# A graph network on one core: queries, edge weights and running sums in SBUF, and a table built in pairs of PSUM banks

## The chip, the core and the metric

One of the eight cores of a Trainium2 chip runs the whole program. Its engines each work through a queue of their own in order: PE (matrix products), DVE (vector work), ACT (copies and functions of single elements), POOL (here it issues the DMAs whose addresses come from a list of rows, and nothing else of weight) and SP (plain DMAs). Products land in PSUM, 8 banks of 512 float32 for each of 128 partitions; the rest of the working data lies in SBUF. The metric is the device time of one execution in microseconds. Three runs of the kernel before took 4051.14, 4055.07 and 4069.09 us; the median is 4055.07.

## What is computed

Two layers of a heterogeneous graph transformer over 6250 nodes of 16 types and 100000 edges of 32 types, with 8 heads of 16, and then a residual layer norm:

```python
def gt_layer(x, ntype, etype, src, dst, Wk, Wq, Wv, Wa, Watt, Wmsg, pri, skip, g, b):
    k, q, v = (typed_linear(x, ntype, W).reshape(n, H, HS) for W in (Wk, Wq, Wv))
    kT = jnp.einsum('nhd,htdo->nhto', k, Watt)
    vT = jnp.einsum('nhd,htdo->nhto', v, Wmsg)
    a = jnp.einsum('ehd,ehd->eh', kT[src, :, etype], q[dst]) * pri[:, etype].T / SQRT_D
    att = edge_softmax(a, dst, n)
    hag = segment_sum((vT[src, :, etype] * att[:, :, None]).reshape(-1, H * HS), dst, n)
    h = silu(typed_linear(hag, ntype, Wa))
    alpha = sigmoid(skip[ntype])[:, None]
    return layernorm(h * alpha + x * (1 - alpha)) * g + b
out = layernorm(x + (gt_layer(gt_layer(x)) @ ff_w + ff_b))
```

## The kernel before

**The table.** For each layer a table in device memory holds, for every node and each of the 32 edge types, a row of 256 numbers: the node's key and value turned by that type's matrices. An edge then needs one row, (source node, edge type), of 1 KB.

**The stages.** First the nodes are ranked by type and number of incoming edges, in 50 blocks of 128 nodes, while PE builds the first layer's table. Then `edges(0)` runs over superblocks of 3 or 4 blocks: for every block it gathers the rows of its edges, does the attention and sums up, and `nodes` turns the sums into the layer's output. From this output `nodes` makes keys, values and queries of layer 2, and `pieces_of` with `table_block` builds the second layer's table block by block, beside the gathers of later superblocks. Last, `edges(1)` does the same over the second table, with the final layer norm in `nodes` and no table beside it. The other branch, `arm(False)`, handles graphs that don't fit the blocks; it doesn't run here.

**One block of edges.** Rows come in chunks of four edges for each of 128 nodes. POOL issues four gathers for a chunk (L970) into one of twelve `kv` buffers. DVE multiplies the key half by the query (L982), sums it by heads into `a` (L986), and, once all chunks are in, `finished` subtracts the maximum, ACT takes the exponential (L894), and DVE sums the weights (L897), multiplies the value halves by them (L905) and adds the products up in `acc` (L912), which L915 sums over its four slots. `finished` of one block is interleaved with the chunks of the next.

**What lies in PSUM.** For these steps three operands are kept in PSUM: a `qw` tile in one bank (two buffers) holds a block's query, which ACT copies there (`query`, L876), and behind it the weights that ACT writes; `acc` has a bank of its own. Two banks (`nps`) serve the node work and three (`tps`) the tiles `tb` of the table. That is all eight.

**One block of the table.** `table_block` makes, for 16 edge types at a time, a staging tile `st` out of two halves, keys and values. A half is four products, one for each pair of heads, with 32 rows of PE each and 512 columns, each into a bank `tb` of its own; PE does each product in two instructions (L261). ACT copies each bank to `st` (L268); in the last superblock DVE does copies 1 and 3 (L266). When both halves are there, POOL scatters `st` to the table (L1188), three steps later in the program. Each half ends in a `yield`, at which other work is interleaved.

**What sets the order.** The program is written by generators: after each chunk, `tick` advances the node work (`work`) and the table (`pieces`) by as many steps as `spread` planned for the chunk. POOL's queue is kept in the order in which this is written, gathers and scatters mixed. The other engines' queues are put in order by a scheduler, which goes by when it expects operands to be ready. A gather waits for its `kv` buffer to be free, a scatter for ACT's (or DVE's) copies, and layer 2's first gather for all scatters.

Of the kernel before, what the change touches and what calls it, by code (L numbers as in the profile page):

```python
# [18 lines left out]
P = 128  # L19
# [77 lines left out]
def kernel(  # L97
# [54 lines left out]
    typed = dram.tile([NB, P], I32, name="typed")  # L152
# [97 lines left out]
    def table_block(pool, ps_pool, kT, vT, i, share, bufs, store):  # L250


        for tg in range(TG):
            tt = slice(tg * 16, (tg + 1) * 16)
            st = pool.tile([P, 16, 2 * D], F32, name="st", bufs=bufs)
            for half, (yT, bd) in enumerate(((kT, bdk), (vT, bdv))):
                for hp in range(HP):
                    s = slice(hp * 2 * HS, (hp + 1) * 2 * HS)
                    pt = ps_pool.tile([P, SB * P], F32, name="tb").rearrange(
                        "p (t c) -> p t c", t=16)  # L260
                    nc.tensor.matmul(pt, yT[s, i * P:(i + 1) * P], bd[s, tt, :],  # L261
                                     start=True, stop=True)
                    c0 = half * D + hp * 2 * HS
                    to = st[:, :, c0:c0 + 2 * HS]
                    if hp in share:
                        nc.vector.tensor_copy(to, pt)  # L266
                    else:
                        nc.scalar.copy(to, pt)  # L268
                yield
            store(tg, st)  # L270
# [168 lines left out]
    with tc.tile_pool(name="tp", bufs=2) as tp, \  # L439
# [4 lines left out]
        def rank_order():  # L444
# [204 lines left out]
            tyr = pp.tile([NB, P], I32, name="tyr")  # L649
# [119 lines left out]
    def arm(fast):  # L769
# [65 lines left out]
        def edges(l):  # L835
# [38 lines left out]
            def query(s, i):  # L874
                qw = qwp.tile([P, 512], F32, name="qw")
                nc.scalar.copy(qw[:, :D], got[s][0][:, i, :])  # L876
                return qw

            def finished(s, i, chunks, kvt, a, w, sums, den):
# [14 lines left out]
                nc.scalar.activation(w, av, AF.Exp)  # L894
                yield
                yield
                nc.vector.tensor_reduce(den[:, i, :], w.rearrange("p k h -> p h k"),  # L897
                                        axis=AX.X, op=ALU.add)

                acc = accp.tile([P, CH, D], F32, name="acc")  # L900
                for j in range(len(chunks) + 1):
                    if j < len(chunks):
# [5 lines left out]
                            w[:, j0:j1, :].unsqueeze(3).to_broadcast([P, j1 - j0, H, HS]),  # L908
# [29 lines left out]
            qw = query(0, 0)  # L938
            for s, (i0, k, types) in enumerate(sbs):
# [6 lines left out]
                for i in range(k):  # L946
# [17 lines left out]
                    for j0, j1 in chunks:  # L964
# [3 lines left out]
                        for j in range(j0, j1):  # L968
# [14 lines left out]
                            kk, kk, qw[:, :D].unsqueeze(1).to_broadcast([P, c, D]), op=ALU.mult)  # L983
# [14 lines left out]
                    w = qw[:, D:D + K * H].rearrange("p (k h) -> p k h", h=H)  # L998
                    before = finished(s, i, chunks, kvt, a, w, sums, den)
                    qw = then[0] if then else None  # L1000
# [60 lines left out]
        def nodes(l, i0, k, types, sums, den, ntb, table):  # L1061
# [46 lines left out]
            if not last:  # L1108
# [49 lines left out]
                table(pieces_of(i0, k, outs[0], outs[1], (1, 3) if final else ()))  # L1158
# [23 lines left out]
        def pieces_of(i0, k, kT, vT, share):  # L1182
# [182 lines left out]
```

## Time and profile before

| what | value |
|---|---|
| median of 3 runs | 4055.07 us |
| the profiled execution's own time | 4025.79 us |
| its span | 4024.0 us |
| mean granted PE clock | 0.67 |
| busy: PE, DVE, ACT, POOL | 2266.9, 2184.1, 910.9, 1947.0 us |
| gathers (L970) | 1734 |
| scatters of the second table (L1188) | 100 |

Times are microseconds from the span's start. A row of the timeline has start, duration, engine, line, operation, output and inputs, the number of like instructions in a row, and in brackets the engine's idle time before it with what ended that. A row of waits has who waited for whom, then the total, the number of waits and the longest. A row of stretches has, for each engine, its busy time and (x) its instructions, then the granted PE clock, the DMA engines' busy share and what they moved. A row of a group has its number, its busy time, the mean ns of one, and the idle time of the engine just before them.

### The profile page before, as it was taken

How to read it: one execution, taken by the hardware profiler on the slowest of the kernel's cores; microseconds unless marked ns; L12 is line 12 of the kernel's file. 1: busy time of each engine (PE TensorE's matmuls, PEld its weight loads, DVE VectorE, ACT ScalarE, POOL GpSimd, SP SyncE). 2: the span in 40 equal slices, each digit the busy share in tenths (PEclk: the TensorE clock that was granted, in tenths of full speed). 3: DMA queues.
4: the chain of work that ended last, by engine and by line, in shares of the span. 5: the costliest groups of instructions: out<-in, count | busy, mean ns of one | idle time of the engine just before them, and what ended most of it. 6: DMA issues, size and time to landing. Idle time of an engine off the chain costs nothing. (4 is left out here: it accounts for less than half of the span.)

```text
span 4024.0 us, 26100 instructions
## 1 busy us (share of the span) xinstructions
PE 2266.9 (56%) x7142; PEld 1031.4 (26%) x7142; DVE 2184.1 (54%) x4912; ACT 910.9 (23%) x1854; POOL 1947.0 (48%) x2032
## 2 busy tenths in 40 slices
PE   4999998930675578877878889701112112012312
PEld 2444553310232223323333334301111011001111
DVE  4787783335545456545635744244654565555645
ACT  1443434520242123422333245300000000000000
POOL 0000015446465545565455654175666665765663
PEclk9999999955665667666766765555555555555555
DMA  5676647983374435764566567533333332332321
GB/s 137 278 308 273 256 203 307 359 253 93 127 251 163 153 117 206 275 204 147 191 240 213 181 230 273 230 107 90 90 100 92 89 103 86 103 96 86 95 86 44
DMA packets 201152, 697.87 MB, mean 173 GB/s; under 512 B 61332, under 2 KB 110616, under 8 KB 175946
## 3 DMA queue, kind: packets, MB, share of 16 engines
q0 software_dynamic: 105424, 448.83, 33.6%
q1 hardware_dynamic: 72924, 237.40, 15.1%
q10 hardware_dynamic: 22642, 9.82, 1.0%
q8 instruction: 60, 0.98, 0.1%
q14 instruction: 102, 0.84, 0.1%
HBM read 271.40 MB, written 429.49 MB: 174 GB/s over the span
## 5 line engine op out<-in xcount | busy, mean ns | idle before, releaser
L970 POOL DMA_INDIRECT kv<-tab,ell x1734 | 1659.3, 957 | 820.2 <-issue 502.7
L268 ACT COPY st<-tb 128x512 f32<-128x512 f32 x1364 | 740.8, 591 | 978.0 <-PE tb L261 695.8
L261 PE MATMUL tb<-bdv,kvT 32*128 32x512 f32 x800 | 450.3, 988 | 105.8 <-issue 74.2
L261 PE MATMUL tb<-bdk,kvT 32*128 32x512 f32 x800 | 428.1, 960 | 64.9 <-ACT st L268 34.6
L982 DVE TENSOR_TENSOR kv<-kv,qw 128x512 f32<-128x512 f32 (+3 forms) x468 | 297.6, 640 | 306.9 <-DMA kv<-tab,ell 255.1
L731 PE MATMUL l<-xm,wkqv 128*128 128x512 f32 (+1 forms) x832 | 388.0, 601 | 55.9 <-DVE xm L232 54.4
L247 PE MATMUL nb<-ident,hag 128*128 128x128 f32 x100 | 27.6, 418 | 670.2 <-DVE hag L1019 267.6
L1188 POOL DMA_INDIRECT tab<-st,row x100 | 101.3, 1013 | 479.9 <-ACT st L268 413.1
L986 DVE TENSOR_REDUCE a<-kv 128x32 f32<-128x512 f32 (+3 forms) x468 | 296.3, 638 | 64.8 <-remote 35.0
L232 DVE SCALAR_TENSOR_TENSOR xm<-ntb,nb 128x384 f32<-128x384 int32 (+1 forms) x336 | 186.2, 593 | 255.1 <-PE nb L247 163.4
L247 PE MATMUL nb<-ident,hs 128*128 128x128 f32 x100 | 35.4, 458 | 426.0 <-DVE hs L1099 156.1
L912 DVE TENSOR_TENSOR acc<-kv,acc 128x512 f32<-128x512 f32 (+3 forms) x368 | 234.3, 637 | 65.0 <-remote 46.6
L241 PE MATMUL nb<-xm,wa 128*128 128x384 f32 (+1 forms) x384 | 218.3, 729 | 71.6 <-DVE xm L232 27.4
L905 DVE TENSOR_TENSOR kv<-kv,qw 128x512 f32<-128x512 f32 (+3 forms) x368 | 228.1, 627 | 0.0
L266 DVE COPY st<-tb 128x512 f32<-128x512 f32 x220 | 151.1, 687 | 135.5 <-PE tb L261 100.0
L731 PEld LDWEIGHTS l<-xm,wkqv 128*128 128x128 f32 x832 | 149.5, 194 | 288.9 <-issue 201.3
L261 PEld LDWEIGHTS tb<-bdv,kvT 32*128 32x128 f32 x800 | 147.7, 268 | 292.7 <-issue 153.2
L232 DVE SCALAR_TENSOR_TENSOR xm<-ntb,hT 128x512 f32<-128x512 int32 (+1 forms) x208 | 133.9, 658 | 137.8 <-PE l L731 105.9
L261 PEld LDWEIGHTS tb<-bdk,kvT 32*128 32x128 f32 x800 | 146.0, 261 | 235.6 <-ACT st L268 138.4
L247 PEld LDWEIGHTS nb<-ident,hag 128*128 128x128 f32 x100 | 16.5, 207 | 694.2 <-issue 515.1
L719 POOL DMA_DIRECT2D ntb<-in_node_type_dram x13 | 7.3, 560 | 342.5 <-DVE xm L232 342.5
L261 PE MATMUL tb<-bdv,yT 32*128 32x512 f32 x784 | 169.8, 662 | 3.3 <-ACT st L268 2.3
(235 smaller groups left out, 2633.0 us busy)
## 6 DMA issues: line engine op xcount, KB each, us to landing
tab<-st SPq DMA_DIRECT2D x98, 2048.0 KB
kv<-tab,ell POOLq DMA_INDIRECT x1734
ntb<-typed SPq DMA_DIRECT2D x20, 192.0 KB
hr<-xrd SPq DMA_DIRECT2D x20, 192.0 KB
xrd<-xr POOLq DMA_DIRECT2D x11, 256.0 KB
hr<-in_x_dram POOLq DMA_DIRECT2D x10, 256.0 KB
ntb<-in_node_type_dram POOLq DMA_DIRECT2D x10, 256.0 KB
ntb<-typed SPq DMA_DIRECT2D x10, 256.0 KB
```

Of the source, the lines that this page charges most:

```text
L232: nc.vector.scalar_tensor_tensor(xm[:, :n], ntb[:, :n], float(t), hT[:, :n], op0=ALU.is_equal, op1=ALU.mult)
L241: nc.tensor.matmul(ps[:, :n], w[:, t, :], xm[:, :n], start=(t == types[0]), stop=(t == types[-1]))
L261: nc.tensor.matmul(pt, yT[s, i * P:(i + 1) * P], bd[s, tt, :], start=True, stop=True)
L266: nc.vector.tensor_copy(to, pt)
L268: nc.scalar.copy(to, pt)
L731: nc.tensor.matmul(ps[i][:, :n], wkqv[:, i, t, :], xm[:, :n], start=(t == 0), stop=(t == TY - 1))
L905: nc.vector.tensor_tensor((v if j else acc).rearrange("p k (h d) -> p k h d", h=H), v.rearrange("p k (h d) -> p k h d", h=H), w[:, j0:j1, ...
L912: nc.vector.tensor_tensor(acc[:, :j1 - j0], kvt[j - 1][:, :j1 - j0, D:], acc[:, :j1 - j0], op=ALU.add)
L970: get = nc.gpsimd.indirect_dma_start(out=kv[:, j - j0, :], out_offset=None, in_=tabs[l][:], in_offset=bass.IndirectOffsetOnAxis(ap=ell[:, ...
L982: nc.vector.tensor_tensor(kk, kk, qw[:, :D].unsqueeze(1).to_broadcast([P, c, D]), op=ALU.mult)
L986: nc.vector.tensor_reduce(a[:, j0:j1, :], kk.rearrange("p k (h d) -> p k h d", h=H), axis=AX.X, op=ALU.add)
L1188: put = nc.gpsimd.indirect_dma_start(out=tabs[1].rearrange("(n t) c -> n (t c)", t=16), out_offset=bass.IndirectOffsetOnAxis(ap=row2[:, tg ...
```

## The change

The query is read where it lies in SBUF, and `query` no longer copies it; the weights are written over the logits in `a`, in SBUF; `acc` is an SBUF tile. Three banks of PSUM come free. `tps` stays at three buffers, but in the second layer's table (`w=2`) each is now a pair of banks: two products fill it, and one copy of 128x1024 empties it. In the last superblock DVE takes the second pair of each half in place of copies 1 and 3. The node types `typed`, `tyr` and `ntb` (used in the masks of the typed linear layers) become bf16 in place of int32, half the bytes. The first layer's table (`w=1`, pool `tnb` of five banks) and the branch for other graphs keep single banks.

```diff
-    typed = dram.tile([NB, P], I32, name="typed")
+    typed = dram.tile([NB, P], BF16, name="typed")
...
-    def table_block(pool, ps_pool, kT, vT, i, share, bufs, store):
+    def table_block(pool, ps_pool, kT, vT, i, share, bufs, store, w=1):
...
-                for hp in range(HP):
-                    s = slice(hp * 2 * HS, (hp + 1) * 2 * HS)
-                    pt = ps_pool.tile([P, SB * P], F32, name="tb").rearrange(
-                        "p (t c) -> p t c", t=16)
-                    nc.tensor.matmul(pt, yT[s, i * P:(i + 1) * P], bd[s, tt, :],
-                                     start=True, stop=True)
+                for hp in range(0, HP, w):
+                    pt = ps_pool.tile([P, w, SB * P], F32, name="tb").rearrange(
+                        "p b (t c) -> p b t c", t=16)
+                    for b in range(w):
+                        s = slice((hp + b) * 2 * HS, (hp + b + 1) * 2 * HS)
+                        nc.tensor.matmul(pt[:, b], yT[s, i * P:(i + 1) * P], bd[s, tt, :],
+                                         start=True, stop=True)
                     c0 = half * D + hp * 2 * HS
-                    to = st[:, :, c0:c0 + 2 * HS]
+                    to = st[:, :, c0:c0 + w * 2 * HS].rearrange("p t (b c) -> p b t c", b=w)
...
-        if fast:
-            qwp = ctx2.enter_context(tc.tile_pool(name="qwp", bufs=2, space=PSUM))
-            accp = ctx2.enter_context(tc.tile_pool(name="accp", bufs=1, space=PSUM))
...
-            ntb = npl.tile([P, SB * P], I32, name="ntb", bufs=3)
+            ntb = npl.tile([P, SB * P], BF16, name="ntb", bufs=3)
...
             def query(s, i):
-                qw = qwp.tile([P, 512], F32, name="qw")
-                nc.scalar.copy(qw[:, :D], got[s][0][:, i, :])
-                return qw
+                return got[s][0][:, i, :]
...
-                nc.scalar.activation(w, av, AF.Exp)
+                nc.scalar.activation(av, av, AF.Exp)
...
-                nc.vector.tensor_reduce(den[:, i, :], w.rearrange("p k h -> p h k"),
+                nc.vector.tensor_reduce(den[:, i, :], av.rearrange("p k h -> p h k"),
...
-                acc = accp.tile([P, CH, D], F32, name="acc")
+                acc = ep.tile([P, CH, D], F32, name="acc", bufs=1)
...
-                            w[:, j0:j1, :].unsqueeze(3).to_broadcast([P, j1 - j0, H, HS]),
+                            av[:, j0:j1, :].unsqueeze(3).to_broadcast([P, j1 - j0, H, HS]),
...
-                            kk, kk, qw[:, :D].unsqueeze(1).to_broadcast([P, c, D]), op=ALU.mult)
+                            kk, kk, q.unsqueeze(1).to_broadcast([P, c, D]), op=ALU.mult)
...
-                table(pieces_of(i0, k, outs[0], outs[1], (1, 3) if final else ()))
+                table(pieces_of(i0, k, outs[0], outs[1], (2,) if final else ()))
...
-                yield from steps(table_block(ep, tps, kT, vT, i, share, STB, store))
+                yield from steps(table_block(ep, tps, kT, vT, i, share, STB, store,
+                                             2 if fast else 1))
```

POOL's queue holds the same instructions in the same order as before. On the other engines the rows below show what stands there now; the changed kernel's lines are a few off those of before (its L269 is the copy L268, its L262 the product L261, its L890 the exponential L894, its L978, L982, L901 and L908 are L982, L986, L905 and L912).

ACT's queue in layer 1, from one exponential to the next, before (`st<-tb` are the copies of the table, the rest is node work):

```order
L894 ACTIVATE qw<-a 128x120
L268 COPY st<-tb 128x16x32 x6
L876 COPY qw<-q 128x128
L1146 COPY kvT_7794<-nb 128x384
L1146 COPY kvT_7804<-nb 128x384
L812 COPY qT<-nb 128x384
L268 COPY st<-tb 128x16x32
L816 COPY q<-nb 128x384
L268 COPY st<-tb 128x16x32 x5
L812 COPY qT<-nb 128x512
L268 COPY st<-tb 128x16x32 x4
L894 ACTIVATE qw<-a 128x112
```

And the same place now:

```order
L890 ACTIVATE a<-a 128x120
L269 COPY st<-tb 128x2x16x32 x3
L1141 COPY kvT_7704<-nb 128x384
L1141 COPY kvT_7714<-nb 128x384
L810 COPY qT<-nb 128x384
L814 COPY q<-nb 128x384
L269 COPY st<-tb 128x2x16x32 x3
L810 COPY qT<-nb 128x512
L269 COPY st<-tb 128x2x16x32 x2
L890 ACTIVATE a<-a 128x112
```

Sixteen copies became eight of twice the size, the copy of a query is gone, and a copy of the table that stood between two copies of node work has moved behind them.

PE's queue in layer 1, a little later, before (`tb` are the table's products, `hs` the transposes of a superblock's output, `wkqv` the products of keys, values and queries from it):

```order
L261 MATMUL tb<-bdv,kvT_7804 128x512 x4
L261 MATMUL tb<-bdk,kvT_7794 128x512 x3
L247 MATMUL nb<-ident,hs 128x128 x2
L261 MATMUL tb<-bdk,kvT_7794 128x512
L261 MATMUL tb<-bdv,kvT_7804 128x512 x4
L247 MATMUL nb<-ident,hs 128x128
L261 MATMUL tb<-bdk,kvT_7794 128x512
L1141 MATMUL nb<-xm,wkqv 128x384 x8
L261 MATMUL tb<-bdk,kvT_7794 128x512 x3
L1141 MATMUL nb<-xm,wkqv 128x384 x4
```

And now:

```order
L262 MATMUL tb<-bdv,kvT_7714 128x512 x4
L262 MATMUL tb<-bdk,kvT_7704 128x512 x4
L262 MATMUL tb<-bdv,kvT_7714 128x512 x4
L247 MATMUL nb<-ident,hs 128x128 x3
L262 MATMUL tb<-bdk,kvT_7704 128x512 x2
L1136 MATMUL nb<-xm,wkqv 128x384 x8
L262 MATMUL tb<-bdk,kvT_7704 128x512 x2
L1136 MATMUL nb<-xm,wkqv 128x384 x4
```

Halves that were cut into three products and one, or one and three, with other work between them, now stand whole or as two and two; nothing else moved far.

DVE's queue in layer 2, at the end of a superblock, where the next superblock's first query is needed (the multiplication by it stands first), before:

```order
L982 TENSOR_TENSOR kv<-kv,qw 128x4x128 [waits DMASW6_49,DMASW5_49,DMASW7_49,DMASW4_49,Activation_49]
L912 TENSOR_TENSOR acc<-kv,acc 128x128 [waits DVE_49]
L885 TENSOR_TENSOR a<-a,neg 128x96
L915 TENSOR_REDUCE sums<-acc 128x128 [waits DVE_49]
L986 TENSOR_REDUCE a<-kv 128x32
L890 TENSOR_REDUCE m<-a 128x8 [waits DVE_49]
```

And now:

```order
L978 TENSOR_TENSOR kv<-kv,q 128x4x128 [waits DMASW7_49,DMASW6_49,DMAHW5_49,DMASW5_49,DMASW4_49]
L908 TENSOR_TENSOR acc<-kv,acc 128x128 [waits DVE_49]
L881 TENSOR_TENSOR a<-a,neg 128x96
L911 TENSOR_REDUCE sums<-acc 128x128 [waits DVE_49]
L982 TENSOR_REDUCE a<-kv 128x32
L886 TENSOR_REDUCE m<-a 128x8 [waits DVE_49]
```

The order is the same; the multiplication no longer waits for ACT's copy of the query but for the query's own load (DMAHW5), beside the four gathers.

More of the change, by code (lines that the diff above doesn't have):

```diff
@@ L648, in rank_order @@
             yield
-            tyr = pp.tile([NB, P], I32, name="tyr")
+            tyr = pp.tile([NB, P], BF16, name="tyr")
             nc.vector.tensor_copy(tyr, ty_ps)
@@ L874, in query, with finished @@
             def query(s, i):
-                qw = qwp.tile([P, 512], F32, name="qw")
-                nc.scalar.copy(qw[:, :D], got[s][0][:, i, :])
-                return qw
-            def finished(s, i, chunks, kvt, a, w, sums, den):
+                return got[s][0][:, i, :]
+            def finished(s, i, chunks, kvt, a, sums, den):
                 i0, k, _ = sbs[s]
@@ L937, in edges @@
             before = iter(())
-            qw = query(0, 0)
+            q = query(0, 0)
             for s, (i0, k, types) in enumerate(sbs):
@@ L997, in edges @@
                         step(end=True)
-                    w = qw[:, D:D + K * H].rearrange("p (k h) -> p k h", h=H)
-                    before = finished(s, i, chunks, kvt, a, w, sums, den)
-                    qw = then[0] if then else None
+                    before = finished(s, i, chunks, kvt, a, sums, den)
+                    q = then[0] if then else None
             for _ in before:
```

## The prediction

> **What bounds the kernel now.** I read the table of stretches first, then POOL's waits, then the timeline of one half of a table.
>
> ```profile
> core 0: us, PE busy (x) PEld busy (x) DVE busy (x) ACT busy (x) POOL busy (x), PEclk, DMA share, GB/s
> 1040.00:2500.00 1460.00, 1152.00 (x2595) 494.13 (x2596) 764.07 (x1744) 474.48 (x945) 785.64 (x811) 0.66 0.57 200
> 2500.00:2604.00 104.00, 90.57 (x207) 39.56 (x204) 31.36 (x73) 37.49 (x71) 11.79 (x12) 0.58 0.61 246
> 2604.00:4024.00 1420.00, 256.81 (x642) 146.81 (x642) 779.87 (x2082) 57.42 (x174) 876.71 (x916) 0.53 0.31 91
> ```
>
> The three stretches are the steady part of layer 1's edges (with the second layer's table built beside them), its tail, and layer 2's edges. The change leaves the first 1040 us nearly alone. POOL issues every gather, and its cadence is this:
>
> ```profile
> 1637.54 0.94 POOL L970 DMA_INDIRECT kv<-tab,ell  x1 [0.30 <-issue]
> 1649.43 1.01 POOL L1188 DMA_INDIRECT tab<-st,row  x1 [10.94 <-ACT st L268]
> ...
> L970 POOL DMA_INDIRECT kv<-tab,ell x1734 | 1659.3, 957 | 820.2 <-issue 502.7 <-DVE acc L905 121.2 <-DMA tab<-st 52.6
> ```
>
> A gather takes 0.95 us and 0.30 us pass before the next: 1.25 us. In the steady part 811 instructions need 785.64 + 811 x 0.30 = 1029 us of 1460, so 431 us are waits. In layer 2, 916 need 1152 of 1420.
>
> ```profile
> POOL tab L1188 <- ACT st L268: 362.2, 51, 42.5
> POOL kv L970 <- DVE gi L1032: 31.9, 1, 31.9
> POOL kv L970 <- DVE acc L905: 27.4, 4, 21.7
> POOL tab L1188 <- ACT qw L876: 14.2, 4, 7.0
> ```
>
> So in the steady part the waits are nearly all one thing: POOL stands at a scatter of the table (L1188), with all later gathers behind it in its queue, until ACT has emptied the banks. (The second column is the total, then the number, then the longest.) In layer 2 the row of another kind stands:
>
> ```profile
> POOL out_dram L1220 <- DVE o L1174: 97.7, 11, 26.9
> POOL kv L970 <- DVE acc L905: 93.8, 11, 18.2
> ```
>
> There POOL waits for DVE some 190 us, no table is built, and POOL's own cadence sets the rest. Why is ACT late in layer 1? One half (four products of 32 rows, eight PE instructions, two for a product):
>
> ```profile
> 1649.51 2.08 PE L261 MATMUL tb<-bdk,kvT 32*128 32x512 f32 x6
> 1651.61 1.56 ACT L268 COPY st<-tb 128x512 f32<-128x512 f32 x3 [2.46 <-PE tb L261]
> 1652.25 2.07 PE L261 MATMUL tb<-bdk,kvT 32*128 32x512 f32 x2 [0.66 <-ACT st L268]
> 1654.36 0.59 ACT L268 COPY st<-tb 128x512 f32<-128x512 f32 x1 [1.18 <-PE tb L261]
> ```
>
> Three banks take three products side by side in 2.08 us; the fourth has no bank until ACT has emptied one, and then takes as long alone as the three did. PE is held from 1649.51 to 1654.32, ACT done at 1654.95. The mean over the steady part, for this line alone:
>
> ```profile
> 1040.00:2500.00 1460.00, 681.19 (x1439) 258.90 (x1440) 0.66 0.57 200
> 2500.00:2604.00 104.00, 72.32 (x163) 29.70 (x160) 0.58 0.61 246
> ```
>
> 1439 instructions are 180 halves, 3.79 us each; 20 halves in the tail, 3.55 each. PE, 79% busy in its own order, is what ACT and then POOL wait for.
>
> **The change, part by part.** *Pairs of banks.* Now three tiles of two banks: six products fit, so the four of a half run side by side, and the next half's first pair has a place as well. ACT empties a pair at once; no copy of 1024 is in the trace, but these two are:
>
> ```profile
> L1146 ACT COPY kvT<-nb 128x384 f32<-128x384 f32 x16 | 7.7, 479 | 52.7 <-PE nb L1141 41.1 <-issue 8.6 <-remote 3.1
> L1146 ACT COPY kvT<-nb 128x512 f32<-128x512 f32 x8 | 4.7, 586 | 45.7 <-PE nb L1141 25.5 <-remote 20.2
> ```
>
> 128 more elements cost 107 ns, so 1024 cost 586 + 428 = 1014 ns, against two copies of 0.59. A half then holds PE no less than the 2.08 us that six instructions take and ACT 2.03 us; no more than the 3.79 of now. Both ends of the pipe stand near 2.1, so I take 2.3: 180 x 1.49 = 268 us less of PE's queue in the steady part. What this is worth is read at POOL: a scatter needs two halves. If only its own halves count, 51 waits get 2 x 1.49 = 3.0 us shorter, 153 us; if the backlog ahead of them goes as well, all 362.2 + 14.2 = 376 us go. I take **-250 us**, a little under the middle. In the tail, 20 halves by 3.55 - 2.3 = **-25 us**, since PE is busy there for 90.57 of 104. What comes next as a bound in layer 1 is POOL's 1029 us.
>
> *Query copies go, exp stays in SBUF.* A hundred ACT copies (L876) and their waits go.
>
> ```profile
> DVE den L897 <- ACT qw L894: 146.6, 25, 31.8
> DVE kv L982 <- DMA kv<-tab,ell: 128.4, 34, 13.4
> DVE kv L982 <- ACT qw L876: 37.2, 3, 18.0
> ```
>
> These DVE waits shrink (ACT stood behind PE, as above), but DVE is then early for gathers that POOL has not issued: POOL waited for DVE's buffers only 27.4 us (L905) here. Priced 0; between -59 (these 27.4 and the one wait of 31.9) and 0. The query's buffer is now held until DVE's last multiplication, not until ACT's copy: behind its load stand SP's loads of types and old rows. It has two buffers and is asked for a superblock ahead, so 0; without that lead DVE would wait as for L876, 37.2. *Types as bf16* halves loads that are also issued a superblock ahead, hidden behind its gathers: 0, and no wait shown here is for them. The last superblock's copies on DVE (one pair of two instead of copies 1 and 3) carry the same data: 0.
>
> *Operands from PSUM to SBUF.* Four groups change their source or target:
>
> ```profile
> L982 DVE TENSOR_TENSOR kv<-kv,qw 128x512 f32<-128x512 f32 (+3 forms) x468 | 297.6, 640 | 306.9 <-DMA kv<-tab,ell 255.1 <-ACT qw L876 37.2 <-issue 13.9
> L912 DVE TENSOR_TENSOR acc<-kv,acc 128x512 f32<-128x512 f32 (+3 forms) x368 | 234.3, 637 | 65.0 <-remote 46.6 <-issue 11.7 <-DVE kv L905 4.0
> L905 DVE TENSOR_TENSOR kv<-kv,qw 128x512 f32<-128x512 f32 (+3 forms) x368 | 228.1, 627 | 0.0
> L905 DVE TENSOR_TENSOR acc<-kv,qw 128x512 f32<-128x512 f32 x100 | 68.4, 684 | 0.0
> L580 DVE TENSOR_TENSOR rl<-oc,shifts 128x512 f32<-128x512 f32 x10 | 6.8, 682 | 0.0
> L583 DVE TENSOR_TENSOR oc<-oc,ps 128x512 f32<-128x512 f32 x10 | 6.8, 680 | 2.5 <-PE ps L576 2.5
> ```
>
> Their own duration stays: with both inputs in SBUF (L580) 682 ns, with one in PSUM (L583) 680. [...]
>
> What the move does cost stands in POOL's rows. All 1304 now read two operands from SBUF, and where an instruction of that kind runs today, a gather that starts beside it is longer:
>
> ```profile
> 1655.51 0.56 DVE L1019 TENSOR_TENSOR hag<-sums,rd 128x384 f32<-128x384 f32 x1
> 1655.78 1.10 POOL L970 DMA_INDIRECT kv<-tab,ell  x1 [0.30 <-DVE sums L915]
> 2282.05 2.10 DVE L232 SCALAR_TENSOR_TENSOR xm<-ntb,h 128x512 f32<-128x512 int32 x3
> 2282.05 2.10 POOL L970 DMA_INDIRECT kv<-tab,ell  x1 [0.30 <-issue]
> 3062.94 0.86 DVE L1095 SCALAR_TENSOR_TENSOR hs<-hs,mv,gt 128x128 f32<-128x128 f32 x3
> 3063.29 1.07 POOL L970 DMA_INDIRECT kv<-tab,ell  x1 [0.30 <-issue]
> ```
>
> The first gather met L1019 with 0.29 us of it left and lost 0.15 (1.10 against 0.95): the rest of the DVE instruction less 0.14. The second lost 1.15 behind two that followed each other; the third slipped in behind one of three short ones and lost 0.12. [...]
>
> The four groups hold 297.6 + 234.3 + 228.1 + 68.4 = 828.4 us, 414 for each layer, 29% of layer 2's 1420 us. If starts fall at random and a gather gets in behind the first instruction of 0.68 us, a hit loses 0.54²/2/0.68 = 0.21 us: 916 x 0.29 x 0.21 = 56 us in layer 2, 811 x 0.28 x 0.21 = 48 in layer 1. If it waits for the end of a run of three (1.88 us), a hit loses 0.80: 213 and 182. About 15% is absorbed where POOL waits for DVE anyway (190 of 1420): 48 to 181, and 41 to 155. DVE works in bursts and 512 elements leave less of a gap than 128, so I stand above the lower ends: **+80** in layer 2, **+70** in layer 1.
>
> **Sum.** 4025.8 (the profiled execution) - 250 - 25 + 70 + 80 = 3901. The median of the runs shown, 4055.07, lies 29 us above that execution; the change's median is forecast as far above: **3930**.
>
> **Rivals.** *A, the forecast*, 3840 to 4060 with its own terms moved a little: 0.52; 0.05 of it lies within 0.5%, which is about what a measurement of this kernel tells from no change.
> *B, gathers wait for whole runs, slower.* [...] Place: POOL's start of L970, beside L982, L905 and L912. Price at the upper ends +181 and +155; with the low gain of -153 and -25 it gives 4184, timed **4213**. It decides from (250 + 25) / 1727 POOL instructions = 0.16 us lost by each. For: 2282.05 above; against: 3063.29. Chance 0.18.
> *C, pairs do not shorten a half.* The products are bound by PE at the granted clock of 0.66, not by banks, and a half stays at 3.4: -70 and -3; POOL's waits at scatters then hide most of layer 1's loss, +20, and layer 2 has its +80: 4053, timed **4082**. For: the clock in the stretches; against: two instructions took the 2.07 us of six. Chance 0.15, half of it within 0.5%.
> *D, all waits at scatters go*, and gathers lose the least: -376 - 25 + 41 + 48: 3714, timed **3743**. Chance 0.15.
>
> Faster: 0.47 of A and D's 0.15, 0.62. Same: 0.05 and 0.07, 0.12. Slower: B and half of C, 0.26. The range 3740 to 4190 leaves out the outer halves of B and D.
>
> **What would show it.** A half's eight products in one piece of 2.1 us, and copies of 128x1024 near 1.01 us; POOL's waits for L268's copies near 110 us instead of 362; layer 1 from 1040 to its last gather about 180 us shorter. Gathers of mean 1.04 us instead of 0.957, by about 0.09 us; layer 2 near 1500 us. It is wrong if layer 2 grows by over 150 us (B), if the halves stay above 3 us (C), or if POOL's idle time moves to another wait in layer 1, for the buffers that DVE frees.

## The result, and the profile after

The changed kernel takes 3937.39 us (median of 4, 3932.2 to 3939.85) against 4059.61 for the kernel before (median of 4): a ratio of 0.9707, 95% interval 0.9684 to 0.973. The forecast was 3930. The profiled execution took 3932.2 us, its span 3930.4. So the total came out within 8 us; the terms that made it up did not, as the rest of this document shows. The two profiled executions, 4025.79 and 3932.2 us, lie 94 us apart, the medians 122: the account by stages below is good for some 30 us.

The table of stretches of the changed kernel, cut where its stages now end (layer 1's last gather at 2405.5, layer 2's first at 2497.5):

```profile
core 0: us, PE busy (x) PEld busy (x) DVE busy (x) ACT busy (x) POOL busy (x), PEclk, DMA share, GB/s
1040.00:2406.00 1366.00, 884.22 (x2558) 362.06 (x2556) 776.12 (x1712) 408.33 (x532) 854.76 (x818) 0.72 0.60 211
2406.00:2498.00 92.00, 65.83 (x237) 26.24 (x237) 32.93 (x68) 38.93 (x49) 12.99 (x14) 0.74 0.74 300
2498.00:3924.00 1426.00, 256.51 (x642) 146.63 (x642) 803.28 (x2082) 46.03 (x126) 958.61 (x917) 0.53 0.31 89
```

PE's busy time beside layer 1's edges fell by a quarter, POOL's rose in both layers. From here on a stage is measured from gather to gather on POOL: layer 1 from its first to its last gather, the tail from there to layer 2's first, layer 2 from there to the last row written out. Layer 1 went from 1648.4 to 1562.0 us, the tail from 113.3 to 92.0, layer 2 from 1414.8 to 1425.7.

The products and copies of the second table, by the stretches of their line and by ACT's groups:

```profile
1040.00:2500.00 1460.00, 458.71 (x1600) 144.64 (x1600) 0.73 0.61 217
```

```profile
L269 ACT COPY st<-tb 128x1024 f32<-128x1024 f32 x388 | 375.4, 1021 | 355.8 <-remote 102.4 <-PE tb L262 89.2 <-issue 85.5
L269 ACT COPY st<-tb 128x512 f32<-128x512 f32 x588 | 307.6, 595 | 387.3 <-PE tb L262 369.3 <-DMA tab<-st 7.9 <-issue 4.7
```

1600 instructions are 200 halves: 458.71 / 200 = 2.29 us each, as forecast (2.3), and a copy of a pair takes 1.02 us (1.01). The copies of 512 are those of the first layer's table. In the timeline of PE a half is now often one piece of eight, here in 1.43 us; the 78 such pieces of layer 1 and its tail took 1.14 to 3.42 us, 2.04 in the middle:

```profile
1663.84 0.55 PE L247 MATMUL nb<-ident,hs 128*128 128x128 f32 x3
1664.32 1.43 PE L262 MATMUL tb<-bdk,kvT 32*128 32x512 f32 x8
```

What POOL waits for in layer 1's steady part:

```profile
POOL tab L1183 <- ACT st L269: 213.7, 32, 25.4
POOL kv L966 <- DVE gi L1027: 27.3, 1, 27.3
POOL kv L966 <- DVE acc L901: 20.1, 4, 19.2
```

The waits for the table's copies are 32 and 213.7 us; about 110 were expected. And POOL's gathers, in the groups:

```profile
L966 POOL DMA_INDIRECT kv<-tab,ell x1734 | 1806.1, 1042 | 786.2 <-issue 501.0 <-DVE acc L901 91.0 <-DMA tab<-st 56.8
```

Their mean is 1042 ns (1040 was forecast) against 957. Counting only what each gather takes above 0.95 us, layer 1 lost 80 us to it (12 before) and layer 2 85 (3 before). The timeline shows how, at a burst of `finished` in layer 2:

```profile
2869.31 5.46 POOL L966 DMA_INDIRECT kv<-tab,ell  x1 [0.30 <-DVE kv L901]
2869.68 0.68 DVE L901 TENSOR_TENSOR kv<-kv,a 128x512 f32<-128x512 f32 x1
2870.28 0.68 DVE L908 TENSOR_TENSOR acc<-kv,acc 128x512 f32<-128x512 f32 x1
...
2873.50 0.28 DVE L908 TENSOR_TENSOR acc<-kv,acc 128x128 f32<-128x128 f32 x1
2873.70 0.26 DVE L881 TENSOR_TENSOR a<-a,neg 128x104 f32<-128x104 f32 x1
2873.88 1.01 DVE L911 TENSOR_REDUCE sums<-acc 128x128 f32<-128x512 f32 x1
```

The gather stands through ten DVE instructions, all with two operands in SBUF, and ends 0.81 us after the last of them (L881 ends at 2873.96, the gather at 2874.77); L911, which has one, runs beside it. So whole runs of DVE do hold a gather, as rival B feared. But layer 2 has grown by 11 us, not by 82. What POOL waited for in layer 2 shows where the rest went:

```profile
POOL kv L966 <- DVE acc L901: 63.8, 6, 13.8
POOL out_dram L1216 <- DVE o L1169: 61.0, 8, 25.5
```

These two were 93.8 and 97.7 before. In all, POOL's waits for DVE in layer 2 fell from 276 to 193 us, by as much as its gathers grew.

### The profile page after: what moved, and what is told of

It is laid out like the page before. It is cut to its first block, busy times and chain, and to the rows that moved or that the text cites. A ratio compares the mean times of both kernels' runs of the same rounds, so it can differ in the third digit from the quotient of the medians.

```text
span 3930.4 us, 25592 instructions
## 1 busy us (share of the span) xinstructions
PE 1974.2 (50%) x7142; PEld 887.1 (23%) x7142; DVE 2232.3 (57%) x4900; ACT 833.8 (21%) x1366; POOL 2104.1 (54%) x2032
## 5 line engine op out<-in xcount | busy, mean ns | idle before, releaser
L966 POOL DMA_INDIRECT kv<-tab,ell x1734 | 1806.1, 1042 | 786.2 <-issue 501.0
L269 ACT COPY st<-tb 128x512 f32<-128x512 f32 (+1 forms) x976 | 683.1, 764 | 743.1 <-PE tb L262 458.4
L978 DVE TENSOR_TENSOR kv<-kv,q 128x512 f32<-128x512 f32 (+3 forms) x468 | 301.7, 647 | 469.2 <-DMA kv<-tab,ell 426.2
L232 DVE SCALAR_TENSOR_TENSOR xm<-ntb,nb 128x384 f32<-128x384 bf16 (+1 forms) x336 | 186.7, 593 | 245.2 <-remote 158.4
L982 DVE TENSOR_REDUCE a<-kv 128x32 f32<-128x512 f32 (+3 forms) x468 | 297.2, 639 | 29.4 <-remote 6.5
L262 PE MATMUL tb<-bdv,kvT 32*128 32x512 f32 x800 | 276.5, 817 | 43.5 <-ACT st L269 24.8
L262 PE MATMUL tb<-bdk,kvT 32*128 32x512 f32 x800 | 256.4, 814 | 57.8 <-ACT st L269 35.5
L890 ACT ACTIVATE a<-a 128x128 f32<-128x128 f32 (+12 forms) x100 | 31.9, 319 | 1143.3 <-DVE a L888 487.1
L908 DVE TENSOR_TENSOR acc<-kv,acc 128x512 f32<-128x512 f32 (+3 forms) x368 | 233.2, 634 | 57.7 <-remote 47.6
L901 DVE TENSOR_TENSOR kv<-kv,a 128x512 f32<-128x512 f32 (+3 forms) x368 | 231.0, 636 | 0.0
L267 DVE COPY st<-tb 128x512 f32<-128x512 f32 (+1 forms) x208 | 149.2, 718 | 121.9 <-PE tb L262 88.4
L241 PE MATMUL nb<-xm,wq 128*128 128x384 f32 (+1 forms) x192 | 104.3, 704 | 179.4 <-DVE xm L232 159.1
L262 PE MATMUL tb<-bdv,yT 32*128 32x512 f32 x784 | 169.7, 658 | 4.7 <-ACT st L269 3.5
```

The costliest lines, as they stand in the source:

```text
L232: nc.vector.scalar_tensor_tensor(xm[:, :n], ntb[:, :n], float(t), hT[:, :n], op0=ALU.is_equal, op1=ALU.mult)
L241: nc.tensor.matmul(ps[:, :n], w[:, t, :], xm[:, :n], start=(t == types[0]), stop=(t == types[-1]))
L262: nc.tensor.matmul(pt[:, b], yT[s, i * P:(i + 1) * P], bd[s, tt, :], start=True, stop=True)
L901: nc.vector.tensor_tensor((v if j else acc).rearrange("p k (h d) -> p k h d", h=H), v.rearrange("p k (h d) -> p k h d", h=H), av[:, j0:j1, ...
L908: nc.vector.tensor_tensor(acc[:, :j1 - j0], kvt[j - 1][:, :j1 - j0, D:], acc[:, :j1 - j0], op=ALU.add)
L966: get = nc.gpsimd.indirect_dma_start(out=kv[:, j - j0, :], out_offset=None, in_=tabs[l][:], in_offset=bass.IndirectOffsetOnAxis(ap=ell[:, ...
```

## The experiments

Three questions: how the gain divides between the pairs and the moved operands, why layer 2 didn't pay for its longer gathers, and what still holds the table. In the diffs `+` is the experiment and `-` the changed kernel, unless another is named. Each ratio is to the kernel before on the same chip, with its 95% interval. Their stages, in one table at the end of this section, are from one profiled execution each.

**The operands alone** (`operands_only`).

```diff
-                yield from steps(table_block(ep, tps, kT, vT, i, share, STB, store,
-                                             2 if fast else 1))
+                yield from steps(table_block(ep, tps, kT, vT, i, share, STB, store, 1))
-                table(pieces_of(i0, k, outs[0], outs[1], (2,) if final else ()))
+                table(pieces_of(i0, k, outs[0], outs[1], (1, 3) if final else ()))
```

> The second table keeps single banks, three of them as before (copies of 512, DVE's share 1 and 3); query, weights and acc stay in SBUF. A half should take 3.5 to 3.8 us of PE again and its copies 0.59 us. If layer 1 pays its longer gathers in full (+70 on the 1648 us from its first to its last gather), layer 1 takes about 1715 and the profiled execution about 4105. If the waits at the table's scatters (357 us before) hide the longer gathers, layer 1 stays at 1650 to 1665, those waits fall by as much as the gathers grow (to about 290), and the execution is at 4040 to 4055. Layer 2 as in the changed kernel, about 1426, in both.

Measured: 4015.29 us, ratio 0.9917 (0.9884 to 0.9949). The stretch of the table's products:

```profile
1040.00:2560.00 1520.00, 745.90 (x1600) 281.06 (x1600) 0.67 0.59 207
```

A half takes 745.90 / 200 = 3.73 us, as before, and the tail 111.8. Gathers lost 80 and 86 us, as in the changed kernel. Yet layer 1 took 1614 us, 34 less than before, and layer 2 only 7 more, so that neither expectation for layer 1 holds. POOL's waits at scatters, 375 us in the whole of layer 1 before (all for ACT), were 277. So the operands' move, forecast at +150, is worth about -34 by the timed ratio (0.83% of 4052; 21 to 47 by its interval), and the pairs the rest: from 0.9917 to 0.9707, 85 us (94 with the changed kernel's second ratio, 0.9686, below). Why layer 1 gained by the operands is a question of its own; see `qw_sbuf`.

**Six single banks** (`six_single2`): as `operands_only`, with `bufs=6` for `tps`.

> As the changed kernel, but the six banks of the second table are single tiles, emptied by copies of 512 (DVE takes copies 1 and 3 in the last superblock). If the number of banks is what shortened a half, PE's half stays at 2.3 us, and the execution within 10 us of the changed kernel (3937). If one copy for two banks matters (ACT's four copies 4 x 0.59 = 2.36 us against 2 x 1.01 = 2.03), a half goes to 2.4 to 2.6, the waits at scatters rise from 214 by 25 to 60 us, and the execution takes 3960 to 4000.

Measured: 3911.53 us, ratio 0.9734 (0.9678 to 0.979). The half:

```profile
1040.00:2560.00 1520.00, 505.52 (x1600) 219.73 (x1600) 0.71 0.60 214
```

2.53 us. The intervals of this and of the changed kernel overlap: most of what the pairs bring is that six banks are there. The half is that of the second expectation, but the waits at scatters didn't rise (204 us in layer 1, 218 in the changed kernel). One copy for two banks shortens a half by 0.24 us, which the time doesn't show.

**Two pairs** (`two_pairs`): `bufs=2` in place of 3.

> As the changed kernel with two pairs in place of three. A half has just its four products' place, and the next half's first pair waits for a copy. If pairs fill and empty in turn (a pair is filled in about 1.05 us, half of 2.1, and emptied in 1.01), a half stays near 2.3 to 2.5 us and the execution within 15 us of 3937. If products run side by side only when all four have a place at once, two by two take 2.1 us each as six instructions did, a half goes back to 3.5 or more, and with it what the pairs brought, 52 us of layer 1 and 20 of its tail by the run with single banks: about 4010.

Measured: 3953.48 us, ratio 0.9823 (0.9778 to 0.9869), between the two expectations. The half:

```profile
1040.00:2560.00 1520.00, 583.32 (x1600) 169.50 (x1600) 0.68 0.60 212
```

2.92 us, and a tail of 111.7 us. The third pair, which gives the next half a place, is worth 1.2% by the two ratios.

**Two pairs, weights and acc in PSUM** (`two_pairs_w_acc`).

```diff
+            wp = ctx2.enter_context(tc.tile_pool(name="wp", bufs=1, space=PSUM))
+            accp = ctx2.enter_context(tc.tile_pool(name="accp", bufs=1, space=PSUM))
...
-                acc = ep.tile([P, CH, D], F32, name="acc", bufs=1)
+                acc = accp.tile([P, CH, D], F32, name="acc")
```

> Two pairs, and the two banks that this frees hold the weights and acc, in both layers; the query is read from SBUF without a copy. Of 1304 DVE instructions with two operands in SBUF 468 are left, and gathers should lose about 55 us in all instead of 165. If such loss costs time only in part (0.43 of it by the run with acc and weights in PSUM in layer 2: 26 of 59 us), this saves some 45 us, 3890, if two pairs do as well as three; with halves back at 3.5 us about 3960. If the loss stands in layer 1 in full, 55 + 26 = 80 us are saved, 3855.

Measured: 3949.55 us, ratio 0.982 (0.9779 to 0.9861): the same as `two_pairs`. Gathers lost 30 and 25 us in place of 66 and 81. Layer 2 was 39 us shorter and layer 1 38 us longer; the second difference is within the spread of single executions of layer 1 (see `after_again`). The time shows no gain from removing half of the loss there, and neither expectation comes out.

**Layer 2: a query copy put back** (`l2_copy_q`).

```diff
+                if l == 0:
+                    return got[s][0][:, i, :]
+                qc = ep.tile([P, D], F32, name="qc", bufs=2)
+                nc.scalar.copy(qc, got[s][0][:, i, :])
+                return qc
```

> In layer 2 alone ACT copies each block's query again, from SBUF to SBUF, so all operands stay in SBUF and only the copy and its wait come back. If the missing query copies made DVE earlier and so paid for the longer gathers, layer 2 goes from 1426 to about 1490 and the execution to about 4000. If the longer gathers are hidden in POOL's waits for DVE, or DVE's own gaps shrank for another reason, layer 2 stays at 1420 to 1435 and the execution at 3930 to 3945.

Measured: 3939.58 us, ratio 0.9746 (0.9685 to 0.9808); layer 2 took 1431 us, POOL's waits for DVE in it were 194. The missing copies are not what paid.

**Layer 2: weights and acc in PSUM** (`l2_acc_w`). The table's banks are given up after layer 1, and layer 2 uses them.

```diff
+            if l:
+                tctx.close()
+                accp = ctx2.enter_context(tc.tile_pool(name="accp", bufs=1, space=PSUM))
+                wp = ctx2.enter_context(tc.tile_pool(name="wp", bufs=2, space=PSUM))
```

> In layer 2 alone acc and the weights lie in PSUM again, the query is read from SBUF without a copy: 234 instead of 652 of the DVE instructions of layer 2 read two operands from SBUF. Gathers there should lose about 30 us in all instead of 85. If those 85 us stand in the time and something else of the change paid for them, layer 2 goes from 1426 to about 1371 and the execution to about 3882. If POOL's waits for DVE hide them, layer 2 stays at 1412 to 1426 and these waits grow from 194 to about 250.

Measured: 3909.64 us, ratio 0.9656 (0.9619 to 0.9694). Layer 2: gathers lost 26 us in place of 85, POOL's waits for DVE rose to 239, and the stage took 1400 us. Of 59 us less loss 26 reached layer 2's time (37 against the changed kernel's second execution, below): between the expectations. One more thing came back with `acc` and weights in PSUM, about 21 us less work of DVE in its reductions (see the section on the prediction), so the 26 us aren't the gathers' alone.

**Layer 2: all three in PSUM** (`l2_all`): as `l2_acc_w`, and the query copied by ACT to a bank of its own.

> In layer 2 alone query, weights and acc all lie in PSUM, the query copied by ACT as before, but into a tile of its own, so that its copy doesn't wait for the weights of the block before last. Gathers should be back at 0.95 us there. If the tile that query and weights shared is what made DVE late before (POOL's waits for DVE 276 us in layer 2, then 239 without it), layer 2 takes 1380 to 1395 and the execution about 3890. If not, layer 2 is back at 1410 to 1420, as before the change, and the execution at 3920 to 3930.

Measured: 3892.54 us, ratio 0.9663 (0.962 to 0.9707). Gathers lost 3 us, layer 2 took 1406, POOL's waits for DVE were 267. Taking away all 82 us that the operands add to the gathers shortened layer 2 by 20 to 31 (against the two executions of the changed kernel, 1425.7 and 1437.2), DVE's shorter reductions included. DVE's order differs in places between the two kernels, so the next run is the cleaner one.

**Layer 2: POOL made longer by itself** (`pool_delay`): `l2_all` with

```diff
+                        if l:
+                            nc.gpsimd.memset(junk, 0.0)
```

after each chunk's gathers. On PE and ACT every instruction stands in the same order as in `l2_all`, on DVE all but three of 4900, and every operand lies where it did.

> The kernel with all three operands of layer 2 in PSUM, and in layer 2 a memset of 128x256 on POOL after each chunk's gathers (its output is used by nothing): 234 of them, each estimated at 0.3 to 0.4 us, 80 us in all, as much as the gathers lost beside DVE, but at fixed places. If POOL has slack in layer 2, whatever makes it longer, layer 2 goes from 1406 to 1420 to 1440. If only a loss that falls beside DVE's long runs is hidden (because POOL would wait for DVE there), layer 2 goes to about 1480.

Measured: 3937.88 us, ratio 0.9674 (0.9632 to 0.9715); the memsets by POOL's groups, and POOL's waits in layer 2 (of `l2_all` first):

```profile
L996 POOL MEMSET junk<- 128x256 f32 x234 | 77.0, 329 | 8.2 <-remote 6.5 <-issue 1.6
```

```profile
POOL out_dram L1233 <- DVE o L1186: 98.7, 11, 27.6
POOL kv L983 <- DVE acc L918: 88.5, 11, 18.2
```

```profile
POOL out_dram L1236 <- DVE o L1189: 91.1, 11, 27.6
POOL kv L984 <- DVE acc L918: 66.9, 9, 11.3
```

77 us more on POOL made layer 2 13.5 us longer (1419.6 against 1406.1); its waits for DVE fell from 267 to 219, and some of its idle time between issues went too. The same layer 2 took 1425.7 and 1437.2 us in two executions of the changed kernel, so the 13.5 us are good for about 12; that most of the 77 us is hidden is clear of that. It is the first expectation: in layer 2 POOL has slack, whatever makes it longer. What sets layer 2 instead isn't shown.

**The changed kernel again** (`after_again`).

> The changed kernel itself once more, on the chip of the three runs beside it. The stage of layer 1 took 1531 to 1562 us in four executions of the same code, so one execution can't tell less than some 30 us of it; ratio to the kernel before 0.965 to 0.975.

Measured: 3944.0 us, ratio 0.9686 (0.9638 to 0.9734); layer 1 took 1570, the tail 94, layer 2 1437. Seven executions of the table below (the two of the changed kernel, the three `l2_` runs, `pool_delay` and `pe_busy`) have the same layer 1, with DVE's and ACT's instructions in the same order; it took 1531 to 1585 us, so a single execution of layer 1 shows no difference under some 55 us.

**Query and weights in one tile again, in SBUF** (`qw_sbuf`).

```diff
+                qw = ep.tile([P, 512], F32, name="qw", bufs=2)
+                nc.scalar.copy(qw[:, :D], got[s][0][:, i, :])
+                return qw
...
-                nc.scalar.activation(av, av, AF.Exp)
+                nc.scalar.activation(w, av, AF.Exp)
```

> The changed kernel, but query and weights share a tile again, with two buffers and ACT's query copies, as before the change, only that this tile lies in SBUF: the DVE instructions with two operands in SBUF stay as they are. If ACT, standing at a query copy until DVE has used up the weights of the block before last, is what held the table's copies behind it (and what made the moved operands alone 34 us faster in layer 1 in spite of longer gathers), the waits at scatters go from about 205 to 260 or more, layer 1 from about 1543 to 1580 to 1630, and the execution to 3980 to 4030. If not, the execution stays within 20 us of the changed kernel's.

Measured: 3961.94 us, ratio 0.9748 (0.969 to 0.9806) beside 0.9686 in the same series; the waits at scatters are 241 us, with 238 in `after_again`. The intervals overlap. This doesn't show that ACT's copies held the table, nor exclude that they cost a little.

**PE kept at work in layer 2** (`pe_busy`): `l2_acc_w` with six products after each chunk's reduction, into a bank that nothing reads.

> The kernel with acc and weights of layer 2 in PSUM and its query uncopied, and in layer 2 six products on PE after each chunk's reduction, into a bank that nothing reads. Nearly all gaps of DVE before an instruction that waits for nothing but DVE's own last result (329 us in layer 2 there) fall where PE, ACT and SP all stand waiting, and none where PE runs. If PE at work takes them away, they fall below 100 us, and layer 2, where POOL waits 239 us for DVE, from 1400 to 1300 to 1370. If the two only coincide, the gaps stay at 300 or so and layer 2 at 1400 or a little more, since node work stands behind these products on PE.

Measured: 4588.89 us, ratio 1.1326 (1.1267 to 1.1385). Each product is two instructions, which makes PE the bound (1507 of 2074 us busy in layer 2), so the time tells nothing of the question. Something can be read from DVE's gaps (over 0.2 us, before an instruction that waits for nothing but DVE's own last result): 117 us of them are left of the 329 in `l2_acc_w`, 52 us in 34 gaps from 2575 to 2672 alone, and there PE is held as well. Its timeline and DVE's in that phase:

```profile
2602.32 1.01 PE L1001 MATMUL idle<-wa,ident 128*128 128x512 f32 x1 [0.45 <-issue]
2605.13 1.01 PE L1001 MATMUL idle<-wa,ident 128*128 128x512 f32 x1 [1.80 <-issue]
2607.91 1.01 PE L1001 MATMUL idle<-wa,ident 128*128 128x512 f32 x1 [1.78 <-issue]
2610.72 1.01 PE L1001 MATMUL idle<-wa,ident 128*128 128x512 f32 x1 [1.79 <-issue]
```

```profile
2602.32 0.69 DVE L922 TENSOR_TENSOR acc<-kv,acc 128x512 f32<-128x512 f32 x1 [2.50 <-remote]
2606.52 0.70 DVE L922 TENSOR_TENSOR acc<-kv,acc 128x512 f32<-128x512 f32 x1 [1.52 <-DVE kv L915]
2610.72 0.70 DVE L922 TENSOR_TENSOR acc<-kv,acc 128x512 f32<-128x512 f32 x1 [2.91 <-remote]
```

PE's products start 2.8 us apart with nothing that the profile shows to wait for, two of them at the very moment of a late DVE instruction (2602.32, 2610.72). So in these phases an idle PE is not what makes DVE late: both are held. Why two thirds of the gaps went isn't shown, but they kept to one condition. PE's granted clock over layer 2 was 0.81 here (0.53 in the changed kernel), and 0.50 in this phase; of the 117 us, 112 lie where it was at half, which it was for some 780 us of the 2074, and 5 in the 1270 us in which it was full. Which of the two brings the other is open.

**Layer 1: POOL made longer** (`pool_delay1`): the changed kernel with the memset for `l == 0`.

> The changed kernel, and in layer 1 a memset of 128x256 on POOL after each chunk's gathers (nothing uses its output): 234 of 0.33 us by the run with them in layer 2, 77 us. If layer 1, like layer 2, isn't bound by POOL, the waits at scatters (218 and 238 us in two executions of the changed kernel) take most of it and fall to 150 to 180; layer 1 goes from 1562 and 1570 to 1575 to 1595, and the timed execution is 10 to 25 us above the changed kernel's 3937 and 3944. If POOL's time counts in full there, as the forecast's +70 had it, layer 1 takes about 1640, and the timed execution 4015.

Measured: 3888.4 us, ratio 0.9568 (0.9538 to 0.9597). Neither: with 77 us more work on POOL, layer 1 took 1521.9 us, 40 to 48 less, and the tail 82.8; the timed ratio is lower by 48 to 56 us, clear of the intervals. The waits at scatters, here of its steady part:

```profile
POOL tab L1186 <- ACT st L269: 143.0, 24, 31.2
```

But the memsets changed more than POOL. With them the scheduler put 69 of 9242 instructions of PE, 56 of 2601 of ACT and 349 of 8466 of DVE in other places. The largest waits of the changed kernel show what order can do. Its POOL and PE at one of them:

```profile
1417.73 0.95 POOL L966 DMA_INDIRECT kv<-tab,ell  x1 [0.30 <-issue]
1437.30 4.37 POOL L1183 DMA_INDIRECT tab<-st,row  x1 [18.62 <-ACT st L269]
```

```profile
1405.38 1.56 PE L1117 MATMUL nb<-xm,wkqv 128*128 128x384 f32 x4 [1.28 <-issue]
1422.93 11.44 PE L1117 MATMUL nb<-xm,wkqv 128*128 128x384 f32 x28 [15.99 <-ACT kvT L1124]
1434.30 1.13 PE L262 MATMUL tb<-bdv,kvT 32*128 32x512 f32 x4
```

POOL stands 18.62 us at a scatter, not for banks: the trace shows PE idle for 16 us before a superblock's keys, values and queries (L1117), and the table's products stand behind 28 of those instructions. The same scatter with the memsets, and PE there:

```profile
1429.15 0.33 POOL L979 MEMSET junk<- 128x256 f32 x1
1429.65 1.01 POOL L1186 DMA_INDIRECT tab<-st,row  x1 [0.17 <-issue]
```

```profile
1415.56 2.32 PE L1120 MATMUL nb<-xm,wkqv 128*128 128x384 f32 x4 [2.02 <-DVE xm L232]
1417.80 2.07 PE L262 MATMUL tb<-bdv,kvT 32*128 32x512 f32 x2
1419.80 2.93 PE L1120 MATMUL nb<-xm,wkqv 128*128 128x384 f32 x4
```

Node products and table products alternate, and POOL doesn't wait. Whether the other order or the slower pace of gathers did it isn't separated: a run with that order and no memsets wasn't tried. This is the fastest version measured; its interval lies below the changed kernel's.

| kernel | ratio | layer 1 | tail | layer 2 | gathers above 0.95 us: layer 1, layer 2 |
|---|---|---|---|---|---|
| before | 1 | 1648 | 113 | 1415 | 12, 3 |
| changed | 0.9707 | 1562 | 92 | 1426 | 80, 85 |
| changed, again | 0.9686 | 1570 | 94 | 1437 | 71, 82 |
| operands_only | 0.9917 | 1614 | 112 | 1422 | 80, 86 |
| six_single2 | 0.9734 | 1544 | 85 | 1417 | 66, 81 |
| two_pairs | 0.9823 | 1548 | 112 | 1431 | 66, 81 |
| two_pairs_w_acc | 0.982 | 1586 | 106 | 1392 | 30, 25 |
| l2_copy_q | 0.9746 | 1545 | 92 | 1431 | 77, 95 |
| l2_acc_w | 0.9656 | 1533 | 90 | 1400 | 80, 26 |
| l2_all | 0.9663 | 1531 | 92 | 1406 | 63, 3 |
| pool_delay | 0.9674 | 1585 | 94 | 1420 | 70, 3 |
| qw_sbuf | 0.9748 | 1583 | 85 | 1441 | 65, 92 |
| pe_busy | 1.1326 | 1560 | 93 | 2074 | 62, 8 |
| pool_delay1 | 0.9568 | 1522 | 83 | 1424 | 76, 89 |

## Why the prediction was right in sum, and where its steps were not

*Halves, copies, gathers*: right, each within a few per cent (2.29 for 2.3 us, 1.02 for 1.014, gathers of 1042 ns for 1040). Rival C, that pairs don't shorten a half, is out, and with `six_single2` beside it the reason given, too few banks, holds. Not all of it is banks, though. The forecast's floor for a half, 2.08 us, isn't one: pieces of eight took down to 1.14 us. A single instruction takes about 0.6 to 0.7 us or about 1.1 to 1.2, before and after; its mean fell from 974 to 815 ns (950 with two pairs, 830 with six single banks), while PE's granted clock in this stretch rose from 0.66 to 0.73 (0.68 and 0.71). The forecast had no term for that, so the closeness of 2.29 to 2.3 is in part luck.

*-250 for POOL's waits at scatters*: the mechanism was right and the size wrong. The waits fell by 158 us (375 to 218), and 99 of these also went without any pair. What the pairs brought in time was about 85 to 94 us with the tail, a third of the 275 forecast. The step that failed is "if the backlog ahead of them goes as well", and the middle taken from it: the backlog didn't go as a whole. During the 375 us before, PE ran the table's products for 153, other products for 145, and was idle for 77; during the 218 us that are left, for 67, 72 and 78. So more than half of the table's part went and half of the other products', while PE's idle part stayed; the wait at 1437.30 has 13 us of node products in it and 1.6 of the table's. The lower end, -153, lay closer, and even that counted waits as time.

*-25 for the tail*: right, 113 to 92, and it belongs to the pairs (112 in `operands_only`), to the third above all (112 with two).

*+70 and +80 for longer gathers*: the lengthening was right (68 and 82 us more than before), its price wrong. The premise that failed is "POOL's own cadence sets the rest", and with it "about 15% is absorbed". By `pool_delay` 77 us more on POOL cost layer 2 13.5, so over 80% is absorbed; the 82 us of the gathers cost at most the 20 to 31 of `l2_all`, which hold DVE's reductions too. For the same reason rival B, though gathers do wait for whole runs of DVE (5.46 us beside ten instructions), came to nothing: its point of decision, 0.16 us for each POOL instruction, took for granted that each counts.

*Query copies priced at 0*: not contradicted in layer 2 (`l2_copy_q`); in layer 1 open. `operands_only` was 34 us faster in spite of gathers that are 68 us longer. `qw_sbuf` didn't show the copies to be the reason, and since the order on the engines differs too, it stays open what was.

*Operands' own duration unchanged*: right for the four groups named; the products with the query took 680 ns before and 687 now, the weighted values 676 and 686:

```profile
L982 DVE TENSOR_TENSOR kv<-kv,qw 128x512 f32<-128x512 f32 x400 | 271.6, 680 | 275.6 <-DMA kv<-tab,ell 230.1 <-ACT qw L876 37.2 <-issue 7.6
L905 DVE TENSOR_TENSOR kv<-kv,qw 128x512 f32<-128x512 f32 x300 | 200.6, 676 | 0.0
```

```profile
L978 DVE TENSOR_TENSOR kv<-kv,q 128x512 f32<-128x512 f32 x400 | 274.6, 687 | 418.7 <-DMA kv<-tab,ell 385.3 <-issue 33.2
L901 DVE TENSOR_TENSOR kv<-kv,a 128x512 f32<-128x512 f32 x300 | 202.8, 686 | 0.0
```

But two more groups changed their source, and the forecast left them out: the sum of `acc` over its four slots (L915, now L911), and the sum of the weights (L897, now L893: 295 ns before, 395 now).

```profile
L915 DVE TENSOR_REDUCE sums<-acc 128x128 f32<-128x512 f32 x100 | 67.9, 679 | 10.3 <-remote 6.8 <-DVE kv L982 2.5 <-DVE a L986 0.7
L911 DVE TENSOR_REDUCE sums<-acc 128x128 f32<-128x512 f32 x100 | 101.1, 1011 | 5.8 <-DVE a L982 2.1 <-remote 1.8 <-DVE a L881 1.5
```

That is 43 us more of DVE's work, 21 of them in layer 2, where its busy time rose from 779.87 to 803.28 us. In `l2_all`, with `acc` and weights back in PSUM there, the two take 674 and 292 ns in layer 2. What these 43 us cost in time isn't separated.

*The sum*: layer 1 was to be 180 us shorter and layer 2 80 longer; by the profiled executions they were 86 shorter and 11 longer. -275 and +150 were both too large, the first by 181 to 190, the second by 184 (-34 measured for the operands in all). The errors were of one kind: POOL's waits and POOL's work were both counted as time, in stages that POOL doesn't set (`pool_delay` shows this for layer 2; in layer 1 `pool_delay1` agrees, but the order changed with it). That is why they cancelled, and why a total within 8 us is luck and proves little for the terms. Rival D's 3743 would have needed POOL as the bound, too.

## What to carry to other kernels

That an engine is busy or issuing for 80% of a stage doesn't make it what sets the stage: if it also waits for another engine in the same loop, added work can go into those waits (POOL's for DVE in layer 2 fell from 267 to 219 us under 77 us of memsets), and time taken off it can come back as waits (267 us in `l2_all` against 193 in the changed kernel, with 82 us less in its gathers). A cheap test is to add a known amount of useless work to it (77 us here) and see how much comes out (13.5). And where a scheduler orders the queues, look at the order of what a late instruction stands behind before counting buffers: in the five largest waits left here, 95 us in all, PE ran node work for 51, was idle for 23 and ran the table's products for 21.

## What the runs showed of the hardware that was not expected

A gather on POOL can stand behind an unbroken run of DVE instructions with two operands in SBUF: up to 5.7 us in the changed kernel against 0.95, while 1397 of its 1734 gathers stay under 1 us.

A DVE reduction of 512 elements that adds across the four slots of an SBUF tile (L911) took 1.01 us. The same from PSUM took 0.68 (L915 before), and so did one from SBUF along the row (L982 of the changed kernel, 678 ns).

In phases of some 20 to 100 us DVE's instructions start late, half of them by 1.0 to 2.2 us in the changed kernel, though they wait for nothing but DVE's own last result. In layer 2 of the changed kernel:

```profile
2604.53 0.69 DVE L901 TENSOR_TENSOR kv<-kv,a 128x512 f32<-128x512 f32 x1
2607.55 0.69 DVE L908 TENSOR_TENSOR acc<-kv,acc 128x512 f32<-128x512 f32 x1 [2.33 <-remote]
2608.25 0.69 DVE L982 TENSOR_REDUCE a<-kv 128x32 f32<-128x512 f32 x1
2608.86 0.68 DVE L901 TENSOR_TENSOR kv<-kv,a 128x512 f32<-128x512 f32 x1
2611.75 0.69 DVE L908 TENSOR_TENSOR acc<-kv,acc 128x512 f32<-128x512 f32 x1 [2.21 <-remote]
```

Such gaps of over 0.2 us came to 337 us in layer 2 before and 211 now; they were 310 to 350 in the four kernels that have acc and weights of layer 2 in PSUM without added PE work, and 166 to 225 in those that have them in SBUF. Since `l2_acc_w` has 329 us of them and the shorter layer 2, they don't explain the result. `pe_busy` shows PE's instructions late in the same phases and at the same moments. In that run 112 of the 117 us lie where PE's granted clock was at half. Their cause is open.
